# One attention step's second low part behind the softmax, a base activation held back, and graph counts loaded two output units later, in a four-layer graph transformer kernel

## The chip, the cores and the metric

The kernel runs on one core of one Trainium2 chip. The metric is the device time of one execution in microseconds (us). The core has five engines that each run their own queue of instructions in order: PE multiplies matrices, ACT applies functions element by element, DVE and POOL do vector work, and SP issues transfers. Sixteen DMA engines move the data. Some transfers (those of the graph counts here) are issued from POOL's queue.

## The reference

The network adds to `x` a graph transformer of 1024 nodes of width 512 on a graph of 16384 edges: a first graph convolution, four layers, and a last graph convolution.

```python
h = jnp.maximum(_layernorm(x, axis=-1), 0.0)          # the network's input
...
h = _gcn(batch_norm(h), src, dst, gcn_in_w, gcn_in_b, n)
for i in range(L):                                     # L = 4
    a = _attn(_ln(h, ln2_w[i], ln2_b[i]), cond, Wq[i], Wk[i], Wv[i], Wo[i])
    h = h + a
    u = _ln(h, ln3_w[i], ln3_b[i]) @ geglu_w[i] + geglu_b[i]
    val, gate = jnp.split(u, 2, axis=-1)
    h = h + (val * gelu(gate)) @ ffo_w[i] + ffo_b[i]
h = _gcn(h, src, dst, gcn_out_w, gcn_out_b, n)
return x + (h + x_in)                                  # x_in = relu(layernorm(x))
```

Attention works in 16 groups: 64 nodes of a group ask a condition of 256 rows of width 512, in 8 heads of 64. The kernel takes them in pairs and calls each pair a group: a layer has `NG` = 8 of them.

## The kernel before

**Split products.** A float32 operand is split into a high part of twelve bits, a low part and a third part that is their difference. A product is then three matrix products: high by high and low by low add up in one PSUM bank; ACT scales that bank in place (`Twelve`, L381), and the product of the third parts (`as` by `bs`) is added to it afterwards. PE's third group of such a product therefore waits for ACT's scaling. Left operands are split by `left_parts`: ACT writes `ah` (L318), DVE writes `al` from `ah` and the operand (L319), and POOL writes `as` in two halves (L324), or DVE does it (L321) where the caller says so.

**An attention step.** In each layer `l` the loop over `g` runs steps 0 to 6. In step `g` PE computes the keys of group `g+1` (`k`), transposes the probabilities of group `g` (`tr_pr`), multiplies them by the values (`po`, `mix`), and computes the scores of group `g+1` (`sc`, L831). Then the softmax of group `g+1` runs on DVE and ACT in turn: the row maxima `nmax` (DVE, L838), the exponentials `pr` (ACT, L843), reciprocals (DVE, L846) and the scaling `pr` by `inv` (DVE, L848). The last of these scalings is known as `scores.last`. Meanwhile PE computes the values of group `g+1` (`v`), and behind them the product with the output weights (`oy`, `ox`, L903), which needs `oh` (ACT), `ol` and `os` (DVE, L892 and L893).

Each step also splits the condition of group `g+2` (`split_cond`): it lies in two tiles `ct`, of 1024 columns each, so there are two `ah_c`, two `al_c` and four halves of `as_c`. In steps 1 and 2 `base_of` prepares one block each of what is added at the very end: ACT writes `again` (L1557), DVE adds the bias row to the input block and then adds `again` to it (L1559, L1560), and SP stores the result in `base_dram` (L1561).

**The output phase.** A layer ends with 16 output units of 24 matrix products (L1252). Unit `n` multiplies one block of the gated features, read from `f_dram` as tile `fr`, by a block of weights (`wff`, split into `bh_wff`, `bl_wff`, `bs_wff`). Before unit `n`, the code fetches `fr` of `n+2` and splits that of `n+1` into `ah_f`, `al_f`, `as_f`. Weight block `u` is used by units `u` and `u+8`. After certain units other work is put in, by a table called `beside`. In the last layer this is `fetch_counts` (`load_counts`: eight tiles `ce`, issued on POOL, L1383, which the last convolution reads), `fetch_last` (`w_out`, by SP) and `split_last`.

**What sets the order.** A scheduler places the instructions of each engine; dependencies between engines become semaphore waits. `tc.issue_after(x)` adds no wait: it only puts an instruction behind `x` on `x`'s own engine. `waiting_for(x, engine)` is a real wait of that engine for `x`. The large tiles (512 KB) come from one pool of 35 buffers. Tiles get their buffers when the code asks for them, and an instruction that writes a new tile waits until everything that used the old tile in the same buffer has ended. So a block of eight tiles that is asked for earlier takes the buffers that are free earlier, and whatever is asked for behind it gets later ones.

Of the kernel before, what the change touches and what calls it, by code (L numbers as in the profile page):

```python
# [26 lines left out]
def gnn_kernel(  # L27
# [57 lines left out]
    @contextmanager  # L85
    def waiting_for(ins, engine):

        traced = nc.cur_bb.bb.instructions
        n = len(traced)
        yield  # L90
        for i in traced[n:]:
            if i.engine == engine:
                tc.add_manual_dep(i, ins.ins.name, mybir.DependencyInfo(
                    mybir.DependencyClass.Sync, mybir.DependencyReason.DATA))
# [24 lines left out]
    def slots_of(n, name):  # L119
        return [slot(f"{name}_{i}") for i in range(n)]  # L120
# [143 lines left out]
    raw_conds, raw_x = {}, {}  # L264
# [9 lines left out]
    def save_cond(g):  # L274
        for k in range(2):
            nc.sync.dma_start(cond_dram[g][:, 1024 * k:1024 * (k + 1)],
                              raw_x[0, g][k].rearrange("p a b -> p (a b)"))
# [28 lines left out]
    def twelve_bits(t):  # L306
        return t.bitcast(F32R)
# [6 lines left out]
    def left_parts(x, name, t=None):  # L314

        parts = [slots_of(len(x), f"{n}_{name}") for n in ("ah", "al", "as")]
        for h, l, s, x in zip(*parts, x):
            nc.scalar.mul(twelve_bits(h), x, INWARD * TINY)  # L318
            nc.vector.scalar_tensor_tensor(twelve_bits(l), h, -1.0 / TINY, x, OP.mult, OP.add)  # L319
            if t:  # L320
                t.tensor_tensor(twelve_bits(s), h, l, OP.subtract)  # L321
                continue
            for k in range(2):
                nc.gpsimd.tensor_tensor(twelve_bits(s)[:, k, :], h[:, k, :], l[:, k, :],  # L324
                                        OP.subtract)
        return parts
# [16 lines left out]
                        twelve_bits(s)[:, k, :], hk, -TINY, lk, OP.mult, OP.add)  # L343
        return parts

    def split_cond(l, g):
        if g < NG:
            if l == 0:
                save_cond(g)
            conds[g] = left_parts(raw_x.pop((l, g)), f"c_{l}_{g}")  # L350

    conds = {}

# [583 lines left out]
    def load_geglu(l, r):  # L937
        return [load_w(geglu_w[l][:, r * D:(r + 1) * D], f"wval_{l}_{r}"),
                load_w(geglu_w[l][:, DFF + r * D:DFF + (r + 1) * D], f"wgate_{l}_{r}")]
# [485 lines left out]
    for l in range(L):  # L1425
# [90 lines left out]
        def take_ln3():  # L1516
            ln3T.extend(slots_of(2, f"ln3T_{l}_{i}") for i in range(2))
            ln3S.extend(slots_of(3, f"ln3S_{l}"))
            right.extend([ln3T[0][0], ln3T[0][1], ln3T[1][1], ln3S[2], ln3S[0], ln3S[1],
                          ln3T[1][0]])  # L1520
# [62 lines left out]
        for g in range(NG - 1):  # L1583
            if g == NG - 2:
                take_ln3()
                raw = load_geglu(l, 0)
                add_bias(nc.vector)
            if not g:
                probs = scores(l, g, qT, kTs.pop(g))
            if g == NG - 2:  # L1590
                with waiting_for(scores.last, mybir.EngineType.Pool):
                    left = geglu_weights(l, 0, *raw)
            wo_flow = out_parts(l, wo) if not g else iter(())
            wo = next(wo_flow, wo)
            if g in (1, 2):
                fetch_x(2 * l + g - 1)
            k = keys(l, g + 1, wk, 1 if l == 0 and g == 0 else 0)
            for i, u in enumerate(k):
                u.begin()
                if not i:  # L1600
                    for end in ends:
                        end()
                if i > 1:
                    k[i - 2].end()
                next(wo_flow, None)
            k[-2].end()
            for _ in wo_flow:
                pass
            v = values(l, g + 1, wv)
            with in_order(mybir.EngineType.DVE) if g == NG - 2 else nullcontext():  # L1610
                oT = mix(l, g, probs, vs.pop(g), (
                    k[-1].end, nothing, lambda: (v[0].begin(), g == NG - 2 and
                                                 add_bias(nc.vector, *range(4)))))
            if g < NG - 2:
                probs = scores(l, g + 1, qT, kTs.pop(g + 1))
                with tc.issue_after(scores.last.ins):
                    oT = oT()
            if g == NG - 2:
                oT = oT()
                ln3_norm(g - 2, g - 1, behind=mix.last)  # L1620
                add_bias(nc.gpsimd, g - 2, g - 1)
            if g in (1, 2):
                with tc.issue_after(scores.last.ins):
                    base_of(2 * l + g - 1)
            if l == 0:
                fetch_cond(g + 3)
            split_cond(l, g + 2)
            if l:
                load_cond(l, g + 3)
            v[1].begin()  # L1630
            v[0].end()
            v[2].begin()
            v[1].end()
            pieces = attn_out(l, g, oT, wo, pin) if g < NG - 2 else iter(())
            next(pieces, None)
            if g in (3, 5):
                moments_into(mv_kept[:, 2 * (g - 3):2 * (g - 1)], [h[g - 3], h[g - 2]],
                             f"ln3_{l}_{g - 3}")
            if g == NG - 2:
                for nb in range(4):  # L1640
                    ln3_turn(nb, each=pin)
            v[3].begin()
            next(pieces, None)
            v[2].end()
            next(pieces, None)
            ends = [v[3].end]
            if g == NG - 3:
                scale_kept()
            if g == NG - 2:
                for nb in range(4, 6):  # L1650
                    ln3_turn(nb, each=pin)
                for nb in (g - 2, g - 1):
                    ln3_sums(nc.gpsimd, nb)
            if l == 0 and g + 3 < NG:
                turn_cond(g + 3, each=pin)
        g = NG - 1
        f, quads = quads_of(l, 0, left, right)
# [35 lines left out]
        with in_order(mybir.EngineType.DVE):  # L1693
# [3 lines left out]
            of = moments([h[g - 1]], f"ln3_{l}_{g - 1}")  # L1697
# [69 lines left out]
        for r in range(1, R):  # L1767
            f = Gated(l, r)
# [44 lines left out]
        beside = {}  # L1813
        if last:
            hs_out.extend(RowsInTurn(f"hs_{n}_out") for n in ("high", "low"))

            def begin_last():
                for nb in range(4):
                    into_parts(nb)

            def fetch_counts():
                nonlocal again, dinv_row
                again, dinv_row = load_counts()

            def fetch_last():
                nonlocal w_out
                w_out = load_w(gcn_out_w, "w_out")

            def split_last():
                nonlocal w_out  # L1830
                w_out = right_parts(w_out, "w_out")

            beside = {8: begin_last, 9: fetch_counts, 12: fetch_last, 15: split_last}
        else:
            half = range(4), range(4, 8)
            wk, wv = [[], [], []], [[], [], []]

            def fetch_next():
                nonlocal raw_wk
                raw_wk = load_w(Wk[l + 1], f"wk_{l + 1}")  # L1840
                load_cond(l + 1, 0)

            def fetch_values():
                nonlocal raw_wv
                raw_wv = load_w(Wv[l + 1], f"wv_{l + 1}")

            def split_of(to, raw, name, i):
                for part, t in zip(to, right_parts(raw[i:i + 1], f"{name}_{l + 1}_{i}")):
                    part.extend(t)

            def norm_first():
                take_moments(l + 1, half[0], 2)
                ready_first(l + 1, half[0])

            def fetch_more():
                nonlocal wq
                wq = load_w(Wq[l + 1], f"wq_{l + 1}")
                load_cond(l + 1, 1)

            beside = {8: lambda: (fetch_next(), take_moments(l + 1, half[0], 0, 2)),  # L1860
                      9: lambda: split_of(wk, raw_wk, "wk", 0),
                      10: lambda: split_of(wk, raw_wk, "wk", 1),
                      11: lambda: (norm_first(), fetch_values()),
                      12: lambda: split_cond(l + 1, 0),
                      13: fetch_more,
                      14: lambda: split_of(wv, raw_wv, "wv", 0)}
# [42 lines left out]
    for nb in range(NB):  # L1909
        of, at = turned[nb // 4], slice(nb % 4 * P, (nb % 4 + 1) * P)  # L1910
        y, x = bank(f"py_{nb}"), bank(f"px_{nb}")
# [46 lines left out]
```

## Time and profile before

| | us |
|---|---|
| three runs | 2296.37, 2298.52, 2298.68 |
| median | 2298.52 |
| the profiled execution's own time | 2296.64 |
| its span (first to last instruction) | 2294.9 |
| PE busy | 2265.4 (99%) |
| DVE, ACT, POOL busy | 1734.6, 1168.7, 747.1 |

The span is 1.74 us shorter than the profiled execution's own time. Times in rows are us from the span's start. In a timeline a row has the start, the duration, the engine, the line, the operation and its operands (what is written, an arrow, what is read) and, in brackets, how long the engine was idle before it and what released it. Rows of equal instructions are merged (`x4`), and the duration is then that of the group. The names in rows are the program's, without numbers.

### The profile page before, as it was taken

How to read it: one execution, taken by the hardware profiler on the slowest of the kernel's cores; microseconds unless marked ns; L12 is line 12 of the kernel's file. 1: busy time of each engine (PE TensorE's matmuls, PEld its weight loads, DVE VectorE, ACT ScalarE, POOL GpSimd, SP SyncE). 2: the span in 40 equal slices, each digit the busy share in tenths (PEclk: the TensorE clock that was granted, in tenths of full speed). 3: DMA queues.
4: the chain of work that ended last, by engine and by line, in shares of the span. 5: the costliest groups of instructions: out<-in, count | busy, mean ns of one | idle time of the engine just before them, and what ended most of it. 6: DMA issues, size and time to landing. Idle time of an engine off the chain costs nothing. (4 is left out here: it accounts for less than half of the span.)

```text
span 2294.9 us, 34482 instructions
## 1 busy us (share of the span) xinstructions
PE 2265.4 (99%) x12496; PEld 1754.5 (76%) x12496; DVE 1734.6 (76%) x3172; ACT 1168.7 (51%) x2245; POOL 747.1 (33%) x647
## 2 busy tenths in 40 slices
PE   8999999999999999999999999999999999999999
PEld 5678887587887888488887888578788888668777
DVE  9886556999986555989987554989987554899965
ACT  7555445565355445465356444556437444556521
POOL 1121213486021224377021222368112112268301
PEclk9999999999999999999999999999999999999999
DMA  6042211234411101133521111133531111043551
GB/s 206 2 152 70 74 61 42 83 120 152 169 46 65 61 29 42 60 119 99 200 92 65 51 38 42 42 107 100 184 138 56 37 52 51 1 129 111 184 173 57
DMA packets 144113, 204.42 MB, mean 89 GB/s; under 512 B 11240, under 2 KB 68912, under 8 KB 143936
## 3 DMA queue, kind: packets, MB, share of 16 engines
q1 hardware_dynamic: 141840, 196.72, 26.0%
q0 software_dynamic: 1376, 4.30, 0.6%
q8 instruction: 103, 1.69, 0.3%
q10 hardware_dynamic: 720, 1.11, 0.1%
q14 instruction: 74, 0.61, 0.1%
HBM read 151.75 MB, written 50.34 MB: 88 GB/s over the span
## 5 line engine op out<-in xcount | busy, mean ns | idle before, releaser
L324 POOL TENSOR_TENSOR as_c<-ah_c,al_c 128x512 fp32r<-128x512 f32 x128 | 197.7, 1574 | 901.0 <-DVE al_c L319 679.9
L1123 ACT ACTIVATE g<-g 128x512 f32<-128x512 f32 x192 | 112.5, 586 | 152.8 <-PE g L1109 151.5
L381 ACT ACTIVATE k<-k 128x512 f32<-128x512 f32 x125 | 73.0, 585 | 193.0 <-PE k L370 193.0
L1252 PE MATMUL fx<-bs_wff,as_f 128*128 128x512 f32 x512 | 159.0, 390 | 0.6 <-DVE as_f L321 0.6
L1252 PE MATMUL fy<-bl_wff,al_f 128*128 128x512 f32 x512 | 158.8, 390 | 0.6 <-DVE al_f L319 0.5
L318 ACT ACTIVATE ah_f<-fr 128x1024 fp32r<-128x1024 f32 x64 | 67.9, 1061 | 177.3 <-PE fy L1252 98.8
L1252 PE MATMUL fy<-bh_wff,ah_f 128*128 128x512 f32 x512 | 157.8, 390 | 0.2 <-ACT ah_f L318 0.2
L386 DVE COPY kT<-k 128x512 f32<-128x512 f32 x54 | 37.2, 689 | 156.8 <-PE k L370 156.8
L370 PE MATMUL v<-bh_wv,ah_c 128*128 128x512 f32 x508 | 140.9, 399 | 0.0
L370 PE MATMUL v<-bs_wv,as_c 128*128 128x512 f32 x508 | 137.1, 393 | 2.6 <-ACT v L381 2.6
L1050 POOL TENSOR_TENSOR gsa<-gha,gla 128x512 fp32r<-128x512 f32 x96 | 124.1, 1315 | 40.2 <-DVE gla L1045 40.2
L370 PE MATMUL v<-bl_wv,al_c 128*128 128x512 f32 x508 | 136.6, 390 | 0.0
L843 ACT ACTIVATE pr<-sc,nmax 128x256 f32<-128x256 f32 x256 | 118.1, 474 | 35.0 <-DVE nmax L838 34.5
L370 PE MATMUL k<-ah_c,bh_wk 128*128 128x512 f32 x500 | 135.1, 392 | 0.0
L381 ACT ACTIVATE v<-v 128x512 f32<-128x512 f32 x127 | 75.0, 591 | 116.9 <-PE v L370 116.9
L370 PE MATMUL k<-as_c,bs_wk 128*128 128x512 f32 x500 | 132.1, 395 | 1.8 <-ACT k L381 1.8
L370 PE MATMUL k<-al_c,bl_wk 128*128 128x512 f32 x500 | 133.8, 389 | 0.0
L1109 PE MATMUL g<-gr,gha 128*128 128x512 f32 x384 | 120.0, 394 | 0.0
L1109 PE MATMUL g<-gr,gsa 128*128 128x512 f32 x384 | 119.9, 393 | 0.0
L1109 PE MATMUL g<-gl,gla 128*128 128x512 f32 x384 | 118.3, 389 | 0.0
L370 PEld LDWEIGHTS v<-bs_wv,as_c 128*128 128x128 f32 x508 | 93.2, 188 | 27.7 <-ACT v L381 5.7
L370 PEld LDWEIGHTS v<-bh_wv,ah_c 128*128 128x128 f32 x508 | 92.6, 188 | 27.9 <-issue 9.2
(321 smaller groups left out, 5814.3 us busy)
## 6 DMA issues: line engine op xcount, KB each, us to landing
f_dram<-fT SPq DMA_DIRECT2D x128, 256.0 KB, 2.1
fr<-f_dram SPq DMA_DIRECT2D x64, 512.0 KB, 4.1
ct<-cond_dram SPq DMA_DIRECT2D x48, 512.0 KB, 4.7
wff<-in_L_gnn_ffo_w_dram SPq DMA_DIRECT2D x32, 512.0 KB, 5.2
gxb<-in_L_gnn_geglu_w_dram SPq DMA_DIRECT2D x96, 128.0 KB, 2.5
gxa<-in_L_gnn_geglu_w_dram SPq DMA_DIRECT2D x96, 128.0 KB, 2.6
cond<-in_L_gnn_cond_dram SPq DMA_DIRECT2D x32, 256.0 KB, 4.2
cond_dram<-ct SPq DMA_DIRECT2D x16, 512.0 KB, 3.3
```

The costliest lines, as they stand in the source:

```text
L318: nc.scalar.mul(twelve_bits(h), x, INWARD * TINY)
L324: nc.gpsimd.tensor_tensor(twelve_bits(s)[:, k, :], h[:, k, :], l[:, k, :], OP.subtract)
L370: pin(nc.tensor.matmul(self.bank, twelve_bits(left[k // 2])[:, k % 2, self.c * P:(self.c + 1) * P], twelve_bits(right[k // 2])[:, k % 2, : ...
L381: nc.scalar.mul(self.bank, self.bank, 1.0 + TINY)
L386: nc.vector.tensor_copy(self.to(), self.bank)
L843: nc.scalar.activation(pr3[:, a, :], ps3[:, a, :], AF.Exp, bias=nmax[:, a:a + 1], accum_out=tot[:, a:a + 1])
L1050: split_left.last = pin(t.tensor_tensor(s_at, h_at, l_at, OP.subtract))
L1109: pin(nc.tensor.matmul(to, self.part(i, which)[:, k, :], self.rights[i][which].bitcast(F32R)[:, k, :], start=start and k == 0, stop=stop a ...
L1123: pin(nc.scalar.mul(to, to, 1.0 + TINY))
L1252: pin(nc.tensor.matmul(to, twelve_bits(left[which][0])[:, k, b * P:(b + 1) * P], twelve_bits(right[which])[:, k, :], start=u == 0 and whic ...
```

## The change

Three edits.

1. `split_cond` takes a further argument and splits the condition tile by tile. In step 0 of each layer the second tile's split is asked for behind `scores.last`, an order on DVE alone: it concerns the second `al_c`. Tiles are asked for in another order too (`ah`, `al`, `as` of the first tile, then of the second).
2. In steps 1 and 2 `base_of` also makes ACT wait for `scores.last`, so `again` cannot run before the softmax of its step has ended on DVE.
3. In the last layer's output phase `fetch_counts` stands behind unit 11 and no more behind unit 9.

```diff
-    def split_cond(l, g):
+    def split_cond(l, g, behind=None):
         if g < NG:
             if l == 0:
                 save_cond(g)
-            conds[g] = left_parts(raw_x.pop((l, g)), f"c_{l}_{g}")
+            conds[g] = [[], [], []]
+            for i, x in enumerate(raw_x.pop((l, g))):
+                with tc.issue_after(behind.ins) if behind and i else nullcontext():
+                    for to, of in zip(conds[g], left_parts([x], f"c_{l}_{g}_{i}")):
+                        to.extend(of)
...
             if g in (1, 2):
-                with tc.issue_after(scores.last.ins):
+                with tc.issue_after(scores.last.ins), \
+                        waiting_for(scores.last, mybir.EngineType.Activation):
                     base_of(2 * l + g - 1)
             if l == 0:
                 fetch_cond(g + 3)
-            split_cond(l, g + 2)
+            split_cond(l, g + 2, None if g else scores.last)
...
-            beside = {8: begin_last, 9: fetch_counts, 12: fetch_last, 15: split_last}
+            beside = {8: begin_last, 11: fetch_counts, 12: fetch_last, 15: split_last}
```

The order of PE's instructions is the same in both programs, and so is that of POOL's.

**DVE in step 0 of the third layer (`l` = 2).** `al_c_2_0` and `al_c_2_1` are the two low parts of group 2's condition, the rows from `nmax_1_0` to `pr_1_3` are the softmax of group 1, `ol_0` and `os_0` belong to the output product of group 0. Before:

```order
L319 SCALAR_TENSOR_TENSOR al_c_2_0_26153<-ah_c_2_0_26151,ct_2_0_25873 128x1024
L319 SCALAR_TENSOR_TENSOR al_c_2_1_26154<-ah_c_2_1_26152,ct_2_1_25874 128x1024
L838 TENSOR_REDUCE nmax_1_0_26109<-sc_1_0_26089 128x2
L838 TENSOR_REDUCE nmax_1_1_26119<-sc_1_1_26090 128x2
...
L848 TENSOR_SCALAR pr_1_3_26141<-pr_1_3_26141,inv_1_3_26145 128x256 x2
L892 SCALAR_TENSOR_TENSOR ol_0_26086<-oh_0_26085,po_0_26009 128x512
L893 TENSOR_TENSOR os_0_26087<-oh_0_26085,ol_0_26086 128x512
L386 COPY v_1_0_26183<-v_1_1_26169 128x512
```

And after:

```order
L319 SCALAR_TENSOR_TENSOR al_c_2_0_0_26152<-ah_c_2_0_0_26151,ct_2_0_25873 128x1024
L842 TENSOR_REDUCE nmax_1_0_26109<-sc_1_0_26089 128x2
L842 TENSOR_REDUCE nmax_1_1_26119<-sc_1_1_26090 128x2
...
L852 TENSOR_SCALAR pr_1_3_26141<-pr_1_3_26141,inv_1_3_26145 128x256 x2
L896 SCALAR_TENSOR_TENSOR ol_0_26086<-oh_0_26085,po_0_26009 128x512
L319 SCALAR_TENSOR_TENSOR al_c_2_1_0_26159<-ah_c_2_1_0_26158,ct_2_1_25874 128x1024
L897 TENSOR_TENSOR os_0_26087<-oh_0_26085,ol_0_26086 128x512
L390 COPY v_1_0_26183<-v_1_1_26169 128x512
```

The second low part stood directly ahead of the softmax; it now stands behind it, between `ol_0` and `os_0`. The same holds in the other three layers.

**ACT in the same layer.** `again` is ACT's part of `base_of`, `oh_0` of the output product, and the rows `pr_` are the exponentials. In step 0, before:

```order
L881 COPY pT_0_2_26029<-tr_pr_0_2_26024 128x512
L1557 ACTIVATE again_26440<-x_again_26234,x_shift,x_root 128x512
L381 ACTIVATE v_1_0_26043<-v_1_0_26043 128x512
L318 ACTIVATE ah_c_2_1_26152<-ct_2_1_25874 128x1024
L889 ACTIVATE oh_0_26085<-po_0_26009 128x512
L843 ACTIVATE pr_1_0_26111,tot_1_0_26112<-sc_1_0_26089,nmax_1_0_26109 128x256 x2
```

After, that `again` stands in step 1, behind the exponentials of group 2:

```order
L847 ACTIVATE pr_2_3_26430,tot_2_3_26431<-sc_2_3_26381,nmax_2_3_26428 128x256 x2
L385 ACTIVATE v_2_1_26463<-v_2_1_26463 128x512
L392 COPY v_2_0_26477<-v_2_0_26332 128x512
L1561 ACTIVATE again_26440<-x_again_26234,x_shift,x_root 128x512
L385 ACTIVATE v_2_2_26480<-v_2_2_26480 128x512
L385 ACTIVATE v_2_3_26501<-v_2_3_26501 128x512
```

Each `again` moves one step later (the second one from step 1 to step 2), and now stands ahead of the scaling of the third quarter of that step's values. On DVE the bias addition (L1559) of steps 1 and 2 moves from ahead of `os` to behind it. On SP, in layers 1 to 3, the load of the bias row (which waits for `scores.last` of step 0) now stands ahead of the two `ct` loads of group 3; in layer 0 the loads of two condition groups stand ahead of the stores to `base_dram` in steps 1 and 2.

**SP in the last output phase.** The numbers behind the tiles' names count the tiles in the order in which they are asked for. Before, the eight `ce` tiles have the numbers 35168 to 35175, between `fr_11` and `fr_12`:

```order
L1211 DMA fr_11_35136<-f_dram 128x2x512 [waits DMAHW0_49,DVE_49,DMAHW4_49,PE_49,Activation_49]
L1211 DMA fr_12_35189<-f_dram 128x2x512 [waits DMAHW5_49,PE_49]
L1211 DMA fr_13_35221<-f_dram 128x2x512 [waits DMAHW6_49,PE_49]
L1211 DMA fr_14_35253<-f_dram 128x2x512 [waits DMAHW7_49,DMAHW5_49,DVE_49]
L126 DMA w_out_35285<-in_L_gnn_gcn_out_w_dram 128x2x512 [waits PE_49]
```

After, they have the numbers 35232 to 35239, between `fr_13` and `fr_14`:

```order
L1215 DMA fr_11_35136<-f_dram 128x2x512 [waits DMAHW0_49,DVE_49,DMAHW4_49,PE_49,Activation_49]
L1215 DMA fr_12_35168<-f_dram 128x2x512 [waits DMAHW7_49,DMAHW5_49,PE_49]
L1215 DMA fr_13_35200<-f_dram 128x2x512 [waits DMAHW1_49,DVE_49,DMAHW6_49,PE_49,Activation_49]
L1215 DMA fr_14_35253<-f_dram 128x2x512 [waits PE_49]
L126 DMA w_out_35285<-in_L_gnn_gcn_out_w_dram 128x2x512 [waits PE_49]
```

The order of SP's and POOL's transfers stays; what each waits for changes with its buffer. Which tile's buffer a new one takes, and with which unit that buffer comes free, follows from the order of asking:

| new tile | buffer before, free after | buffer after, free after |
|---|---|---|
| `fr_12` | `bs_wff_1`, unit 9 | `as_f_8`, unit 8 |
| `ah_f_11` | `bh_wff_2`, unit 10 | `bs_wff_0`, unit 8 |
| `al_f_11`, `as_f_11` | `ah_f_10`, `al_f_10`, unit 10 | `fr_10`, `bh_wff_1`, unit 9 |
| `fr_13` | `bl_wff_2`, unit 10 | `ah_f_9`, unit 9 |
| `ce` (eight) | units 8 and 9 | `as_f_9` to `as_f_10`, units 9 and 10 |
| `fr_14` | `fr_12`, once that is split | `bs_wff_2`, unit 10 |

## The prediction

> **What bounds the kernel now.** I read the page first, for the bound:
>
> ```profile
> PE 2265.4 (99%) x12496; PEld 1754.5 (76%) x12496; DVE 1734.6 (76%) x3172; ACT 1168.7 (51%) x2245; POOL 747.1 (33%) x647
> ```
>
> PE is busy 99% of the span of 2294.9 us (its granted clock is 1.00 in the stretches below). So only what makes PE wait counts, and PE time saved or lost anywhere goes into the end nearly one to one. The change touches no PE instruction. I therefore went next to PE's waits, and looked for those that stand where the three edits work (who waited, for whom, us in all, times, longest):
>
> ```profile
> PE v L370 <- ACT v L381: 2.6, 5, 1.0
> ...
> PE fx L1252 <- DVE as_f L321: 0.6, 1, 0.6
> PE fy L1252 <- DVE al_f L319: 0.5, 1, 0.5
> ```
>
> There are two places: values waiting for ACT's scaling, and one output unit waiting for its split operand. A waiting PE also restarts at a slower pace, so the cost is read from stretches of time. The stretches from one `sc` of an attention step to the next show it; rows in pairs, step 0 and then step 1 of layers 0 to 3 (columns: stretch, its length, PE busy and its instructions, clock, DMA share, GB/s):
>
> ```profile
> 179.14:212.67 33.53, 32.55 (x240) 1.00 0.22 72
> 212.67:244.95 32.28, 32.28 (x241) 1.00 0.24 83
> 717.31:748.57 31.26, 30.80 (x224) 1.00 0.14 43
> 748.57:779.09 30.52, 30.52 (x224) 1.00 0.17 52
> 1246.12:1277.38 31.26, 30.80 (x225) 1.00 0.13 44
> 1277.38:1307.84 30.46, 30.46 (x225) 1.00 0.16 53
> 1774.84:1806.08 31.24, 30.78 (x225) 1.00 0.13 43
> 1806.08:1836.54 30.46, 30.46 (x225) 1.00 0.16 53
> ```
>
> Step 1 does the same work on PE and has no wait at all (busy equals length). Step 0 is longer by 1.25, 0.74, 0.80 and 0.78 us: 3.57 us in all. And in the last output phase, units 9 to 11:
>
> ```profile
> 2199.23:2204.67 5.44, 5.44 (x25) 1.00 0.89 269
> 2204.67:2210.51 5.84, 5.60 (x25) 1.00 1.06 349
> 2210.51:2217.81 7.30, 6.18 (x24) 1.00 1.02 371
> ```
>
> Two units take 5.84 and 7.30 us where the one ahead of them takes 5.44 without a wait: 0.40 + 1.86 = 2.26 us.
>
> **Edit 1: the second low part.** Step 0 of layer 2, and behind it the same rows of step 1, from the timeline:
>
> ```profile
> 1242.99 1.22 DVE L319 SCALAR_TENSOR_TENSOR al_c<-ah_c,ct 128x1024 fp32r<-128x1024 f32 x1
> 1244.35 2.52 POOL L324 TENSOR_TENSOR as_c<-ah_c,al_c 128x512 fp32r<-128x512 f32 x2 [18.41 <-DVE al_c L319]
> 1245.85 2.11 DVE L319 SCALAR_TENSOR_TENSOR al_c<-ah_c,ct 128x1024 fp32r<-128x1024 f32 x1 [1.64 <-ACT ah_c L318]
> 1247.88 1.28 DVE L838 TENSOR_REDUCE nmax<-sc 128x2 f32<-128x512 f32 x2
> 1252.66 0.59 ACT L381 ACTIVATE v<-v 128x512 f32<-128x512 f32 x1
> 1253.30 1.21 PE L370 MATMUL v<-bs_wv,as_c 128*128 128x512 f32 x4 [0.46 <-ACT v L381]
> ...
> 1278.51 1.29 DVE L838 TENSOR_REDUCE nmax<-sc 128x2 f32<-128x512 f32 x2 [1.45 <-PE sc L831]
> 1283.17 0.60 ACT L381 ACTIVATE v<-v 128x512 f32<-128x512 f32 x1
> 1283.94 1.07 PE L370 MATMUL v<-bs_wv,as_c 128*128 128x512 f32 x4
> ```
>
> In step 1 the maxima start 1278.51 - 1277.38 = 1.13 us after `sc`, released by `sc` itself. In step 0 they start 1.76 us after it (1247.88 - 1246.12), right behind `al_c`. ACT's scaling of the values stands behind the exponentials and so ends 7.13 us after `sc`, against 6.39 in step 1 (1283.77 - 1277.38), while an unhindered PE wants it at 6.56 (1283.94). With `al_c` behind the softmax, step 0 should look like step 1: the maxima 0.63 us earlier, the scaling ended 0.17 us before PE asks. The gain is at most the 3.57 us above; in layer 0 the delay is larger and so is the excess. If the margin of 0.17 us is missed by 0.1 in each layer, 3.2 us; if the scaling stays late for another reason, 0. I take 3.57, since step 1 is the measured case with the same work and the same margin.
>
> What the moved instruction now holds up is `os`, the values' copy on DVE, and POOL's `as_c`. What PE needs of them, in the same layer:
>
> ```profile
> 1254.31 0.69 DVE L893 TENSOR_TENSOR os<-oh,ol 128x512 fp32r<-128x512 f32 x1
> ...
> 1258.95 1.09 PE L903 MATMUL ox<-os,os 128*128 128x512 f32 x4
> ...
> 1260.80 1.07 PE L370 MATMUL k<-al_c,bl_wk 128*128 128x512 f32 x4
> ...
> 1266.24 1.07 PE L370 MATMUL k<-as_c,bs_wk 128*128 128x512 f32 x4
> ```
>
> The softmax being 0.63 us earlier, `os` would start at 1253.68 without `al_c` and at 1254.9 with it, and end by 1255.6. PE, 0.8 us earlier than before, takes it at 1258.15: 2.5 us to spare. `al_c` itself ends near 1254.9 and is asked for at 1260.0; POOL's two halves then end at about 1257.5 and are asked for at 1265.4. So the move costs nothing here. That cover would be gone if `os` came over 2.5 us later than this.
>
> [...] The row: `al_c` takes 1.22 us alone and 2.11 us when POOL's `as_c` runs beside it. [...]
>
> **Edit 2: `again`.** It occupies ACT as before, eight times 0.8 us, but a step later, and waits for DVE's softmax. Step 1, before:
>
> ```profile
> 1283.58 0.62 DVE L848 TENSOR_SCALAR pr<-pr,inv 128x256 f32<-128x256 f32 x2
> 1284.16 0.61 ACT L381 ACTIVATE v<-v 128x512 f32<-128x512 f32 x1
> 1288.51 1.07 PE L370 MATMUL v<-bs_wv,as_c 128*128 128x512 f32 x4
> 1290.98 0.81 ACT L1557 ACTIVATE again<-x_again,x_shift,x_root 128x512 f32<-128x512 f32 x1 [2.54 <-DMA x_again<-in_x_dram]
> ```
>
> Its new place is ahead of the scaling at 1284.16, which is the third quarter's. DVE's last scaling of the softmax (first row) ends at about the same time, so the wait is met when ACT arrives. The scaling queued behind it then ends near 1285.7, and PE adds the third part of that quarter at 1288.51: nearly 3 us to spare. Where `again` stood before, it was off PE's path too, even with a wait of 2.54 us for its input, which is loaded in time for the later place. On SP the two `ct` loads of group 3 now stand behind the bias load, which waits for the end of the softmax. In layer 2 they were issued at 1246.00:
>
> ```profile
> 1246.00 0.79 SPq L283 DMA_DIRECT2D ct<-cond_dram  x2
> ```
>
> The softmax ends ahead of `os`, so they come at most 8 us later, and the data are split in step 1, whose `sc` is at 1277.38. Price 0; if the margin failed, up to 0.8 us in each of eight steps.
>
> **Edit 3: the counts.** Units 10 and 11 wait because `ah_f`, `al_f` and `as_f` of unit 11 get buffers that only unit 10 sets free:
>
> ```profile
> 2198.57 0.36 SPq L1211 DMA_DIRECT2D fr<-f_dram  x1
> 2209.40 1.06 ACT L318 ACTIVATE ah_f<-fr 128x1024 fp32r<-128x1024 f32 x1 [9.82 <-PE fy L1252]
> ```
>
> ACT idles 9.82 us until PE's `fy` of unit 10 has ended, and PE then waits for this and the two DVE operations behind it. After the change these buffers come free with units 8 and 9: `fr_11` is issued at 2198.57 (first row) and lands 3.5 us later, `ah_f` can be written at once, `as_f` when unit 9 has ended (2204.67), so by 2205.9, and unit 11 would start at 2210.11. That is 4 us to spare, so the 2.26 us go.
>
> What is late next? The `fr` transfers beside the counts (`fr_11` ahead of the counts, `fr_12` among them; then the eight `ce`, their first reader and their landing):
>
> ```profile
> fr<-f_dram SPq DMA_DIRECT2D x1, 512.0 KB, 3.5
> ...
> fr<-f_dram SPq DMA_DIRECT2D x1, 512.0 KB, 8.0
> ...
> L767 PEld LDWEIGHTS agg_out<-ce,hs_high_out x64: 186/188/188, 2239.3 to 2268.5; 128*128 128x128 f32 x64
> ...
> L1383 POOL DMA_DIRECT2D ce<-c_dram x8: 527/547/578, 2199.9 to 2206.3; - x8
> ...
> DMA to landing us min/median/max: 6.3/7.5/11.8
> ```
>
> The counts' issues run from 2199.9 to 2206.3 now; with buffers of units 9 and 10 they run from about 2204.7 to 2210.7 and land by 2222.5 at the slowest rate seen. They are first read near 2237 (2239.3 less 2.26). `fr_14` gets its buffer with unit 10 (2210.1) and at 8.0 us lands at 2218.1; unit 14 starts at 2226.4 (2204.67 and four units) and needs it at most 3.6 us before (`ah_f` 1.06, and two DVE operations of the size of `al_c`, 1.22): 4.7 us to spare. `fr_15` behind unit 11 (2215.6) lands by 2223.6 and is needed by 2228.3. Nothing becomes late. Bounds: 0 if a transfer takes the gain back, 2.26 if none does; I take 2.26, being over 4 us away from the point where it turns.
>
> **Sum.** 3.57 + 0 + 2.26 = 5.83 us less. The profiled execution took 2296.64, so it would take 2290.8. It stands 1.88 us under the median of the runs, near the fastest of them; against the median 2298.52 the forecast is 2292.7.
>
> **Rivals.**
> *One gain only.* Either the scaling in step 0 stays late (its margin is 0.17 us, the thinnest in this argument) and 2.26 remain: 2296.3; or the counts' stream takes back what units 10 and 11 gave, and 3.57 remain: 2295.0. For it speaks the DMA share of 1.02 to 1.06 in the stretches above, which leaves no room there; against it that the later transfers have 4.7 us.
> *The edits do nothing.* PE's next wait sits right behind the removed one, for instance on `ah_c` or a bank, and both gains vanish: 2298.5. Against it: step 1 has the same chain of work and no wait.
> *Slower: `al_c` in front of `os`.* DVE's queue in step 0 after the softmax now holds `ol`, `al_c`, `os` and the copy of the values. If `al_c` is held by something (its `ah_c`, POOL's work beside it, a buffer freed late, since tiles are asked for in another order), `os` is late for `ox`. It decides once `os` comes over 2.5 us later than worked out; each further us costs 4, one a layer. At 5 us late, 2.5 beyond what is to spare, it costs 10 and the time is 2298.5 - 2.3 - 3.6 + 10 = 2302.6. Against it: `ah_c` has long been written (DVE waited for it at 1245.8), and PE wants `al_c` only at 1260.
>
> **Chances.** Both gains, within 1 us: 0.66. One gain: 0.18. Nothing: 0.08. Slower by this or by late transfers: 0.08. About 0.2%, 4.6 us, is what a measurement of this kernel can tell from no change, and the forecast of 5.83 us lies only 1.2 beyond it, while the three runs spread by 2.3. So of the likeliest case some 0.08 falls within 0.2%, and a little of the others beyond it: faster 0.60, within 0.2% 0.33, slower 0.07. The likeliest case's own range is 2290 to 2294 (2296.37 - 5.83 = 2290.5 at the fastest run, 2298.68 - 4.8 = 2293.9 at the slowest with 1 us missing). The range that should hold 8 in 10 goes from 2289.5 to 2297.5, which takes in one gain only.
>
> **What would show it.** In the profile after: `v` waiting for ACT in step 0 is gone from PE's waits, and the stretches from `sc` to `sc` of steps 0 and 1 are equal; `al_c` takes 1.22 us in its new place and `ox` doesn't wait for `os`; `again` has no wait on a DMA; all sixteen output units take 5.44 us, and `fr` of units 14 and 15 land before their split is due. I am wrong if PE waits in step 0 for `os`, for values or for the next keys, or in units 12 to 15 for `ah_f`.

## The result, and the profile after

| | before | after |
|---|---|---|
| median of 8 runs each, us | 2297.34 | 2290.85 |
| lowest and highest | 2296.16 to 2298.68 | 2290.27 to 2291.20 |
| ratio, 95% interval | | 0.9971 [0.9962, 0.9980] |
| the profiled execution's own time | 2296.64 | 2290.68 |
| span | 2294.9 | 2288.9 |

The change saves 5.96 us between the two profiled executions and 6.49 us between the medians. The medians differ by more because the runs of this kernel lie in two groups about 2 us apart, and four of the eight before but none of the eight after lay in the upper one; what the groups are is told near the end.

PE still bounds the kernel. From the page of the changed kernel:

```profile
PE 2263.5 (99%) x12496; PEld 1755.6 (77%) x12496; DVE 1732.5 (76%) x3172; ACT 1170.5 (51%) x2245; POOL 748.4 (33%) x647
```

The stretches from one `sc` to the next in the changed kernel, step 0 and then step 1 of layers 0 to 3 (stretch, length, PE busy and its instructions, clock, DMA share, GB/s):

```profile
179.46:211.69 32.23, 32.23 (x240) 1.00 0.22 75
211.69:243.93 32.24, 32.24 (x241) 1.00 0.24 83
716.09:746.60 30.51, 30.51 (x225) 1.00 0.11 44
746.60:777.09 30.49, 30.49 (x224) 1.00 0.17 52
1244.03:1274.51 30.48, 30.48 (x224) 1.00 0.13 45
1274.51:1304.99 30.48, 30.48 (x224) 1.00 0.16 53
1771.91:1802.39 30.48, 30.48 (x224) 1.00 0.11 44
1802.39:1832.87 30.48, 30.48 (x224) 1.00 0.16 53
```

Step 0 is now as long as step 1 in every layer, and PE is busy all of it. Against before it lost 1.30, 0.75, 0.78 and 0.76 us: 3.59 us. Units 1, 10 and 11 of the last output phase, in the same view:

```profile
2151.44:2157.44 6.00, 6.00 (x25) 1.00 1.00 340
2200.96:2206.40 5.44, 5.44 (x25) 1.00 0.88 285
2206.40:2211.84 5.44, 5.44 (x25) 1.00 0.97 318
```

Units 10 and 11 lost 0.40 and 1.86 us, 2.26 us together. The two sums make 5.85 of the span's 6.0 us; the other 0.15 us I did not follow. Unit 1 is the one sign of the prediction that did not come: it takes 6.00 us in place of 5.44, with PE busy all the time. It did so before (6.03 us).

The split of unit 11 in the changed kernel, from the timeline:

```profile
2198.63 1.06 ACT L318 ACTIVATE ah_f<-fr 128x1024 fp32r<-128x1024 f32 x1 [2.75 <-DMA fr<-f_dram]
...
2201.05 1.23 DVE L321 TENSOR_TENSOR as_f<-ah_f,al_f 128x1024 fp32r<-128x1024 f32 x1
```

`ah_f` now waits for the landing of `fr_11` and no more for PE. `as_f` is written as soon as unit 9 has ended (2200.96) and is done at 2202.28, 4.1 us before unit 11 starts, as worked out.

Step 0 of layer 2 in the changed kernel, from the timeline:

```profile
1245.16 1.29 DVE L842 TENSOR_REDUCE nmax<-sc 128x2 f32<-128x512 f32 x2 [3.04 <-PE sc L835]
...
1249.83 0.59 ACT L385 ACTIVATE v<-v 128x512 f32<-128x512 f32 x1
1250.59 1.09 PE L374 MATMUL v<-bs_wv,as_c 128*128 128x512 f32 x4
...
1251.36 1.22 DVE L319 SCALAR_TENSOR_TENSOR al_c<-ah_c,ct 128x1024 fp32r<-128x1024 f32 x1
1252.50 0.68 DVE L897 TENSOR_TENSOR os<-oh,ol 128x512 fp32r<-128x512 f32 x1
...
1252.81 2.77 POOL L324 TENSOR_TENSOR as_c<-ah_c,al_c 128x512 fp32r<-128x512 f32 x2 [8.02 <-DVE al_c L319]
1256.09 1.09 PE L907 MATMUL ox<-os,os 128*128 128x512 f32 x4
```

The maxima are released by `sc` itself, 1.13 us after it. ACT's scaling ends at 1250.42 and PE goes on at 1250.59 without a wait. `al_c` takes 1.22 us in its new place, and `os` ends 2.9 us before PE asks for it.

### The profile page after: what moved, and what is told of

Same layout as the page of the kernel before. It is cut to its first block, busy times and chain, and to the rows that moved or that the text cites. A ratio compares the mean times of both kernels' runs of the same rounds, so it can differ in the third digit from the quotient of the medians.

```text
span 2288.9 us, 34504 instructions
## 1 busy us (share of the span) xinstructions
PE 2263.5 (99%) x12496; PEld 1755.6 (77%) x12496; DVE 1732.5 (76%) x3172; ACT 1170.5 (51%) x2245; POOL 748.4 (33%) x647
## 5 line engine op out<-in xcount | busy, mean ns | idle before, releaser
L842 DVE TENSOR_REDUCE nmax<-sc 128x2 f32<-128x512 f32 x128 | 83.0, 679 | 44.0 <-PE sc L835 44.0
```

The source lines that it names most:

```text
L842: nc.vector.tensor_reduce(nmax, ps3, AX.X, OP.max, negate=True)
```

## The experiments

All comparisons are with runs of the kernel before on the same chip. Ratios stand with their 95% intervals.

**Edit 1 alone.** The diff is that of `split_cond` and of its call.

> Edit 1 alone (the second low part of step 0 behind the softmax, tiles asked for one by one). My theory: the whole gain of the attention steps comes from here, 3.6 us less than before (1.25 + 0.74 + 0.80 + 0.78), the stretches from sc to sc of steps 0 and 1 are equal in all layers, and units 10 and 11 of the last output phase still take 5.84 and 7.30 us. Rival: edit 2 is needed for it (ACT's base activation stands in step 0), and this alone brings under 1 us. On the spread: before's runs lie in two groups, near 2296.3 and near 2298.4, while the changed kernel's lie within 0.9 us. If the second group comes from the transfers beside units 10 to 12, this kernel still has the two groups; if it comes from step 0, it has one.

Measured: 2293.34 us against 2296.94, 3.60 us less; ratio 0.9984 [0.9975, 0.9993]. Step 0 of the four layers and units 10 and 11, in its stretches:

```profile
179.27:211.53 32.26, 32.26 (x240) 1.00 0.21 75
715.95:746.45 30.50, 30.50 (x225) 1.00 0.15 44
1243.96:1274.46 30.50, 30.50 (x224) 1.00 0.13 45
1772.02:1802.54 30.52, 30.52 (x225) 1.00 0.14 44
2201.16:2207.00 5.84, 5.60 (x25) 1.00 1.08 342
2207.00:2214.24 7.24, 6.11 (x24) 1.00 0.97 348
```

The whole gain of the attention steps comes with this edit, and the output units keep their wait. Three of its eleven runs lie above 2295, eight below 2293.8: two groups.

**Edit 2 alone.**

```diff
-                with tc.issue_after(scores.last.ins):
+                with tc.issue_after(scores.last.ins), \
+                        waiting_for(scores.last, mybir.EngineType.Activation):
                     base_of(2 * l + g - 1)
```

> Edit 2 alone (ACT's base activation waits for the softmax of its step). My theory: only layer 0 gains, since only there the activation stands ahead of the second ah_c: ah_c 0.7 us earlier, al_c 0.6 earlier, the softmax 0.6 earlier, so 0.6 us less in all; in layers 1 to 3 nothing. Rival: the activation is what delays step 0 everywhere, and this alone brings over 2 us. Two groups of runs as before.

Measured: 2296.74 against 2296.94, ratio 0.9998 [0.9989, 1.0007]: no difference. Layer 0's step 0 became 0.23 us shorter (33.30 against 33.53), not 0.6, and its timeline shows why the rest did not come:

```profile
177.93 6.00 POOL L324 TENSOR_TENSOR as_c<-ah_c,al_c 128x512 fp32r<-128x512 f32 x4 [18.21 <-PE v L370]
...
180.23 1.29 DVE L838 TENSOR_REDUCE nmax<-sc 128x2 f32<-128x512 f32 x2
...
182.67 1.66 DVE L848 TENSOR_SCALAR pr<-pr,inv 128x256 f32<-128x256 f32 x2
...
186.59 1.20 PE L370 MATMUL v<-bs_wv,as_c 128*128 128x512 f32 x4 [0.78 <-ACT v L381]
```

The maxima start 1.13 us after `sc` (179.10), as early as they ever do, and PE still waits 0.78 us. In between, two scalings that take 0.60 to 0.68 us elsewhere took 1.66, while POOL worked through four halves of `as_c`. So the place of `al_c` was not all of it. This led to a second theory: POOL beside DVE is what delays step 0.

**Edit 3 alone.**

```diff
-            beside = {8: begin_last, 9: fetch_counts, 12: fetch_last, 15: split_last}
+            beside = {8: begin_last, 11: fetch_counts, 12: fetch_last, 15: split_last}
```

> Edit 3 alone (counts behind unit 11). My theory: 2.26 us less than before, all sixteen output units take 5.44 us but the second, and step 0 keeps its waits. Rival: the counts' stream takes some of it back at units 13 to 15, under 1 us gained. If the two groups of before's runs come from the transfers beside units 10 to 12, this kernel's runs lie in one group and the median gains 2.3 to 3.3; if not, they keep two groups 2 us apart.

Measured: 2294.53 against 2296.94, 2.41 us less; ratio 0.9989 [0.9980, 0.9998]. Layer 0's step 0 keeps its wait and units 10 and 11 lose theirs:

```profile
179.81:213.32 33.51, 32.53 (x241) 1.00 0.21 72
2204.82:2210.26 5.44, 5.44 (x25) 1.00 0.91 287
2210.26:2215.70 5.44, 5.44 (x25) 1.00 0.95 285
```

Three of its eleven runs still lie above 2295.5, the others at 2294.1 to 2294.9, so the upper group of runs is not only made beside units 10 to 12.

**Edits 1 and 2 without 3.**

> Edits 1 and 2 without 3. My theory: the same as edit 1 alone, 3.6 us less than before, since with the low part behind the softmax the activation ahead of ah_c delays nothing any more. Rival: edit 2 adds to edit 1, 0.6 us or more beyond edit 1 alone.

Measured: median 2294.55, ratio 0.9986 [0.9977, 0.9995]. Seven of the eleven runs lie in the upper group, so the median can't be set against that of edit 1 alone; the lower groups can: 2292.88 to 2293.51 here, 2292.64 to 2293.78 there. Edit 2 adds nothing to edit 1.

**Only the order of asking for tiles.** `split_cond` as changed, called as before (`split_cond(l, g + 2)`).

> Only the other order in which split_cond asks for its tiles (ah, al, as of the first tile, then of the second), in all steps, without any order behind the softmax. My theory: within 0.3 us of before, step 0 still 0.7 to 1.3 us longer than step 1. Rival: part of edit 1's 3.6 us comes from the buffers, and this kernel gains over 1 us. A second question is the two groups of runs, about 2 us apart: in one execution of edit 2 alone PE ran at half pace for 3 us (granted clock 0.54) right behind the wait of unit 11. If that is the second group, this kernel, which keeps the wait, has both groups.

Measured: 2297.67 against 2297.86, ratio 0.9999 [0.9990, 1.0008]. Step 0 keeps its excess in all layers (33.52, 31.25, 31.26 and 31.25 us). The buffers have no part in the gain of edit 1.

**POOL's third parts later, `al_c` where it was.** This is the kernel before with the order of DVE unchanged:

```diff
-            split_cond(l, g + 2)
+            split_cond(l, g + 2, None if g else lambda: waiting_for(
+                scores.last, mybir.EngineType.Pool))
...
         if late:
             with late():
                 for h, l, s in zip(*parts):
                     for k in range(2):
                         nc.gpsimd.tensor_tensor(twelve_bits(s)[:, k, :], h[:, k, :], l[:, k, :],
                                                 OP.subtract)
```

> The kernel before, with one thing changed: in step 0 of each layer POOL's third parts of the condition wait for the end of the softmax; the second al_c keeps its place ahead of the softmax. In the run of edit 2 alone the maxima of layer 0 started in time, yet two pr scalings took 1.66 us beside POOL. My new theory: it is POOL beside DVE that delays step 0. Then the second al_c takes 1.22 us in place of 2.0 to 2.1, ends before sc lets the maxima start in layers 1 to 3, and step 0 loses all of its 0.74 to 0.80 us there, and most of 1.25 in layer 0: 2.3 to 3.6 us less than before, nearly as much as edit 1. Rival: the place of al_c in DVE's queue is what counts, and at most 0.2 us a layer is gained. [...]

Measured: 2293.31 against 2297.86; ratio 0.9983 [0.9974, 0.9992], that of edit 1 alone. Its stretches of step 0 in the four layers:

```profile
179.86:212.13 32.27, 32.27 (x241) 1.00 0.24 75
716.56:747.04 30.48, 30.48 (x224) 1.00 0.12 44
...
1244.41:1274.89 30.48, 30.48 (x225) 1.00 0.15 45
1772.41:1802.89 30.48, 30.48 (x225) 1.00 0.15 44
```

And the timeline of layer 2, whose `sc` is at 1244.41:

```profile
1244.13 1.23 DVE L319 SCALAR_TENSOR_TENSOR al_c<-ah_c,ct 128x1024 fp32r<-128x1024 f32 x1 [1.64 <-ACT ah_c L318]
1245.53 1.29 DVE L846 TENSOR_REDUCE nmax<-sc 128x2 f32<-128x512 f32 x2 [0.17 <-PE sc L839]
...
1251.48 5.50 POOL L332 TENSOR_TENSOR as_c<-ah_c,al_c 128x512 fp32r<-128x512 f32 x4 [27.22 <-DVE pr L856]
1251.86 1.47 DVE L901 TENSOR_TENSOR os<-oh,ol 128x512 fp32r<-128x512 f32 x1
1256.46 1.09 PE L911 MATMUL ox<-os,os 128*128 128x512 f32 x4
```

The second `al_c` stands ahead of the maxima as before, but takes 1.23 us in place of 2.11 and ends 0.17 us before `sc` lets them start. So in layers 1 to 3 the place in DVE's queue alone makes no wait: it takes POOL's work beside `al_c`. In layer 0 another part comes from ACT. There the second `ah_c` came late in the kernel before, and `al_c` with it:

```profile
179.57 1.99 DVE L319 SCALAR_TENSOR_TENSOR al_c<-ah_c,ct 128x1024 fp32r<-128x1024 f32 x1 [1.75 <-ACT ah_c L318]
```

Even at 1.22 us it would have ended at 180.79, some 0.5 us after `sc` lets the maxima start (179.14 + 1.13); this is an estimate from these rows. In the kernel with POOL later the scheduler also set that `ah_c` ahead of the value scaling, so this run does not separate the two parts of layer 0. The price of the collision moved to `os`: 1.47 us in place of 0.69, where 3 us were to spare.

**The counts behind unit 10.**

```diff
-            beside = {8: begin_last, 11: fetch_counts, 12: fetch_last, 15: split_last}
+            beside = {8: begin_last, 10: fetch_counts, 12: fetch_last, 15: split_last}
```

> The changed kernel with the counts behind unit 10. My theory: unit 11's split still gets early buffers, so units 10 and 11 keep 5.44 us; fr_13 now gets a buffer of unit 10 (about 2206 here) and lands 8 to 10 us later, 2214 to 2216, while unit 13 starts at 2217.3 and needs it 3 us ahead of that: a wait of 0 to 2 us in unit 13. So 0 to 2 us more than the changed kernel. Rival: any place behind unit 9 is as good, no difference.

Measured: 2292.66 against 2297.86, ratio 0.9979 [0.9970, 0.9988]; its lower group begins 1 us above that of the changed kernel (2291.24 against 2290.27; the kernel before began at 2295.93 and 2296.16 beside them). Units 12 and 13 in its stretches, and then the wait inside unit 13 from the timeline:

```profile
2211.83:2217.27 5.44, 5.44 (x25) 1.00 1.07 392
2217.27:2223.47 6.20, 5.76 (x25) 1.00 0.44 167
```

```profile
2218.81 0.73 PE L1256 MATMUL fx<-bs_wff,as_f 128*128 128x512 f32 x2 [0.44 <-DVE as_f L321]
```

`fr_13` landed at 2215.1, and the wait moved to unit 13, at 0.76 us. One unit earlier is too early.

**The counts behind unit 13.** The same line with 13.

> The changed kernel with the counts behind unit 13. My theory: fr_14 and fr_15 are asked for ahead of the counts and land sooner; the counts are issued at about 2213 to 2219 and land by 2232, just ahead of their first reader at 2233.6. Within 0.5 us of the changed kernel. Rival: the counts arrive late, and PE waits for them at the start of the last convolution, 1 to 4 us more.

Measured: 2291.92 against 2297.86, ratio 0.9973 [0.9963, 0.9984]. All output units from 2 on take 5.44 us, and PE has no wait for the counts. Four of its eight runs lie at 2290.33 to 2290.93 and four at 2292.92 to 2293.14; the lower group is level with the changed kernel.

**The counts behind the last unit.**

```diff
-            beside = {8: begin_last, 11: fetch_counts, 12: fetch_last, 15: split_last}
+            beside = {8: begin_last, 12: fetch_last,
+                      15: lambda: (split_last(), fetch_counts())}
```

> The changed kernel with the counts behind the last output unit. My theory: their buffers come free with units 13 and 14, so they are issued at about 2222 to 2228 and land between 2228 and 2236, beside the loads of the base; the first reader at 2233.6 waits up to 3 us, and the last convolution ends up to 3 us later than in the changed kernel. Rival: no loss, since only the first of the eight tiles is needed at once.

Measured: 2290.37 against 2296.52, ratio 0.9972 [0.9961, 0.9983]: the same as the changed kernel (2290.23 on that chip). My theory was wrong. The counts' issues and their landing in this kernel:

```profile
L1387 POOL DMA_DIRECT2D ce<-c_dram x8: 532/557/578, 2216.8 to 2223.0; - x8
...
DMA to landing us min/median/max: 3.5/6.5/7.8
```

Their buffers came free some 5 us earlier than I had worked out, and the last landing is at most 2223.0 + 7.8 = 2230.8, ahead of the first reader at 2233. So units 11, 13 and 15 all do.

**The changed kernel without edit 2.** The diff of edit 2, taken back.

> The changed kernel without edit 2 (ACT's base activation free to run in step 0). My theory: same as the changed kernel, within 0.3 us (lower group against lower group), since with the low part behind the softmax nothing waits for what the activation delays. Rival: 0.5 us or more slower in layer 0.

Measured: 2291.65, ratio 0.9976 [0.9967, 0.9985], with lowest runs at 2290.14 and 2290.23 (the changed kernel: 2289.83 and 2290.07). Step 0 of layer 0 takes 32.21 us, as with the edit. No loss that can be told apart; the runs of this kernel spread too evenly for more.

**The changed kernel again.**

> The changed kernel again, on the chip of the next three. In the three profiled executions that lay in the upper of the two groups of runs, PE ran at half its pace for about 3 us: twice in the preamble, at about 126 us, behind a wait of 2.0 us for ACT's scaling of the first keys (in the others that wait is 1.4 to 1.9 us and the pace stays), once behind the wait of unit 11. My theory: the changed kernel has lost only the second place, so it has an upper group too, near 2292.7, in a part of its runs, and its lower group stays at 2290.3 to 2291.2. Rival: its runs all lie within 1 us, as the first eight did.

Measured: 2290.23 against 2296.52, ratio 0.9971 [0.9960, 0.9982]. Six runs lie at 2289.83 to 2290.75, one at 2292.13: it has an upper group too, and it is the run that was profiled.

**The query weights' split behind the first keys.** In the preamble PE waits for ACT's scaling of the first keys, which stands behind two parts of the query weights.

```diff
-            for i in range(2):
-                wq.high(i)
-                with waiting_for(rsqrt.last, mybir.EngineType.Pool):
-                    wq.rest(i)
...
-                staggered(units, {2: turn_some, 3: lambda: split_first(0),
+                staggered(units, {1: lambda: wq_of(0), 2: lambda: (turn_some(), wq_of(1)),
+                                  3: lambda: split_first(0),
```

> The changed kernel with one more change, in the preamble: ACT's two high parts of the first layer's query weights, which wait for their load and stand ahead of the scaling of the first keys, are put behind that scaling, with their low and third parts. My theory: PE's wait of 1.4 to 2.0 us for that scaling goes, and with it the half pace that follows it when it is 2.0 us; the runs lie in one group, 0.5 to 2 us below the changed kernel's lower group, or level with it if the norm's transposes behind it are what PE then waits for. Rival: the half pace has nothing to do with that wait, and two groups stay.

Measured: 2290.73 against 2296.52, ratio 0.9974 [0.9964, 0.9984]; eight runs at 2290.62 to 2291.09 and one at 2292.39, so an upper run stays. It does not beat the changed kernel. The wait for the keys is gone and a new one stands some 9 us later; from the timeline:

```profile
121.89 1.07 PE L374 MATMUL k<-as_c,bs_wk 128*128 128x512 f32 x4
...
131.64 1.05 ACT L1298 ACTIVATE ah_wq<-wq 128x1024 fp32r<-128x1024 f32 x1
...
133.23 1.19 PE L374 MATMUL v<-bs_wv,as_c 128*128 128x512 f32 x4 [1.25 <-ACT v L385]
```

There PE waits for ACT again. Directly ahead of that scaling (at 132.59) stands the second high part of the query weights, which this edit itself put there. In the changed kernel it stands elsewhere, and PE waits for no values at this place, and 0.26 us at the next. So most of the new wait is the edit's own; a place for the query weights that makes neither wait was not tried.

## Why the prediction was right, and where it was not

**The sum.** 3.57 was forecast for step 0, 3.59 was measured; 2.26 was forecast for units 10 and 11, 2.26 was measured; 0 for edit 2, which alone gave 0.2 us, within its interval of none. Against its own profiled execution the forecast was 2290.8, and the changed kernel's was 2290.68. The time on record, 2292.7, was taken from the median of three runs, two of which lay in the upper group; that base, and no term of the sum, makes the 1.85 us to the measured median.

**Step 1 as the measured case.** This was the step that carried the forecast: the same work without the wait lies next to the waiting one in the same trace. It held, margin included: ACT's scaling ends 0.17 us before PE asks, as forecast. The other working in the prediction, 0.63 us off a scaling that ended 7.13 us after `sc`, would have left 0.06 us.

**The cause in edit 1 was only half named.** I wrote that the maxima start late because they stand right behind `al_c` in DVE's queue, and that moving it cures this. The size was right and the cure works, but with POOL's work moved away instead, `al_c` can stay and the whole gain comes (ratio 0.9983, against 0.9984 for edit 1). Its 0.89 us of extra time beside POOL (2.11 us against 1.22, which I had quoted) was what made the maxima late in layers 1 to 3. It makes 0.63 of the 0.74 us by which ACT's scaling of the values came late in layer 2 (7.13 against 6.39 us after `sc`). The other 0.11 lies in the softmax: its first pair of `pr` scalings took 0.73 us beside POOL's second `as_c`, against 0.60 in the changed kernel. Moving `al_c` takes away both: the maxima no longer stand behind it, and POOL's second `as_c`, which waits for it, leaves the softmax. For edit 2 the forecast of nothing was right; the 0.6 us that I expected later of edit 2 alone did not come, for the same reason: beside POOL the scalings behind maxima that were in time still took 1.66 us, against 0.60 to 0.68.

**`os` behind `al_c`.** Worked out with 2.5 us to spare, measured with 2.9. In layer 2 of the changed kernel `os` began at 1252.50, ahead of POOL's two halves (1252.81), and took 0.68 us; the halves took 2.77 us, where the first pair of that step took 2.53. In the run with POOL later, POOL began at 1251.48, ahead of `os` (1251.86), and `os` took 1.47 us. Why the one order costs `os` nothing and the other 0.79 us is not shown.

**The counts' stream.** I gave `fr_14` and `fr_15` 8.0 us to land and 4.7 us to spare. They took 8.8 and 10.4; the row of `fr_15` among the transfers, and then its split in the timeline:

```profile
fr<-f_dram SPq DMA_DIRECT2D x1, 512.0 KB, 10.4
```

```profile
2223.10 1.06 ACT L318 ACTIVATE ah_f<-fr 128x1024 fp32r<-128x1024 f32 x1 [5.42 <-DMA fr<-f_dram]
...
2225.53 1.23 DVE L321 TENSOR_TENSOR as_f<-ah_f,al_f 128x1024 fp32r<-128x1024 f32 x1
```

The split ends at 2226.76; unit 15 starts at 2228.16. So 1.4 us were to spare where I had 4.7 (and 2.3 to the first use, when the third kind of product begins 0.9 us into the unit). The term that was mis-sized is the landing time: `fr_15` now shares the engines with the counts' last tiles and with `w_out` (from 2212 to 2214 the counts' queue took 84.8% of the 16 engines' span and that of SP 21.5%, and `w_out` landed after up to 9.7 us, against 5.7 before). Before, with the counts landed and `w_out` beside it, it took 6.5 us. It did not decide here; with the counts one unit earlier the same kind of delay did, at 0.76 us.

**The rivals.** One gain only, no gain and `os` too late: none of them came. In step 0 and in the output units no new wait sat right behind the removed one.

## What to carry to other kernels

Where a loop's first turn is longer than the next on the engine that bounds the kernel, and both do the same work, the difference is the most that can be gained, and the next turn's rows show what the first must look like. When two instructions stand together on two engines and one of them takes longer than alone, ask whether moving either of them does; here moving DVE's or POOL's gave the same (ratios 0.9984 and 0.9983). A block of tiles asked for early from a rotating pool delays those asked for behind it, long before its own data are needed (here by 2.26 us in units 10 and 11): place it by when the buffers around it come free, with a unit on each side tried.

## What the runs showed of the hardware

In five of the fourteen profiled executions PE's granted clock was lower for a stretch behind a wait. In that of edit 2 alone, PE waited 0.24, 0.53 and 0.59 us at the start of unit 11 and then ran pairs of matmuls at 0.85 us where 0.45 is usual; unit 11, and the slow part of it, 3.30 us at a clock of 0.54:

```profile
2210.13:2219.01 8.88, 7.76 (x25) 0.81 0.86 304
2213.60:2216.90 3.30, 3.30 (x9) 0.54 0.90 299
```

That unit took 8.88 us in place of 7.30. In four others (edits 1 and 2 without 3, the counts behind unit 13, the changed kernel again and without edit 2) a slow stretch came in the preamble, behind the wait for the first keys; from 118 to 132 us the clock was 0.88 in each, here with the counts behind unit 13, and 1.00 in the changed kernel's first profile:

```profile
118.00:132.00 14.00, 12.04 (x55) 0.88 1.00 314
```

```profile
118.00:132.00 14.00, 12.45 (x64) 1.00 1.01 315
```

With edits 1 and 2 alone, two groups of four matmuls at 125.30 and 127.01 took 1.91 and 1.72 us there, against 1.08 in the changed kernel's first profile. The wait for the first keys is 1.4 to 2.0 us long, and its length alone does not decide: behind 1.9 us the clock of the stretch was 1.00 in the run with POOL later, behind 1.8 us it was 0.88 in the run without edit 2. Where the clock was 1.00, four matmuls behind a wait still took longer in step 0 of layer 2 before: 1.21 us behind 0.46 us of waiting, against 1.07 in step 1 without a wait. All five profiled executions with such a stretch lie in the upper group of their kernel's runs, and none of the nine without one does. So this is what the two groups are, as far as the profiled executions show; why some runs take it and others not was not settled. The wait for the first keys may not be the only place in the changed kernel: the run with the query weights' split moved no longer has it, and one of its nine executions lay above the others even so; that one was not profiled. What lowers the clock is not shown; in the execution of edit 2 alone it stood behind 1.36 us of waiting in three pieces.
